# Inverse square roots on ScalarE and VectorE in place of GpSimd's power, in a two-layer macaron kernel

## The chip, the cores and the metric

The kernel runs on one core of a Trainium2 chip. Its engines work from queues of their own: TensorE (PE) multiplies matrices, VectorE (DVE) and ScalarE (ACT) do elementwise work and reductions, GpSimd (POOL) does slow elementwise work and starts indirect transfers, SyncE (SP) starts most other transfers. They meet at semaphores. The metric is the device time of one execution in microseconds (us); the time given for a kernel is the median of several runs.

## The reference

The input is 8 sequences of 256 tokens of 128 features, in float32. Six blocks follow one another, each added to the running x: a mixture of experts, attention with 16 heads, the same mixture again, a channel mix, a gated convolution and the channel mix again.

```
x = x + 0.5 * moe(layernorm(x))
x = x + attention(layernorm(x))
x = x + 0.5 * moe(layernorm(x))
x = x + 0.5 * channel_mix(layernorm(x))
x = x + gated_conv(layernorm(x))
x = x + 0.5 * channel_mix(layernorm(x))
```

The change concerns the inverse roots in it:

```
layernorm(x) = (x - mean) / sqrt(var + 1e-5)
rmsnorm(x, w) = x * rsqrt(mean(x * x) + eps) * w
out  = sum over a token's 2 experts of gate * rmsnorm(expert's row)
moe  = rmsnorm(out, out_norm_w) @ W_out.T
channel_mix: r = sigmoid(xr @ W_r); k = relu(xk @ W_k)**2; r * (k @ W_v)
gated_conv: silu for u and v, a long filter by a Fourier transform, u * o @ W_o
```

So the end of each mixture (the combine) needs, for each token, two inverse roots for the two experts' rows, and one for the sum of them; each layer norm needs one.

## The kernel before

The 2048 tokens lie in four chunks of 512 (NCH = 4), each as 4 tiles of 128 tokens (TPC = 4) across the 128 partitions, and stay in on-chip memory as `xs[c]`. Statistics of a chunk are therefore tiny tiles: 128x4 for one number a token, 128x8 for the two experts' factors `cf`.

The stages in time, as the trace has them: the first dispatch of tokens to experts, the experts of layer 0 (to about 184 us), attention's prologue (184 to 206), attention's loop, in which the dispatch of the next mixture is interleaved, the experts of the second mixture (about 419 to 517), and the tail (517 to the end), which holds the combine of the second mixture, the channel mix (`m0`), the gated convolution (`g`) and the channel mix (`m1`).

Order is written by hand. On PE, DVE, ACT and SP the instructions stand in the order in which the Python code issues them (a manual schedule); `power_of` also keeps its instructions on POOL in program order. The steps of different chunks are interleaved as closures:

- `combine` (L694) gives the steps `fetch` (transfer of the experts' rows back), `sums` (L718: cf = mean square + eps, then the power), `added` (L724: cf times gate; the first expert's rows scaled on ACT into acc, L730; the second's added on DVE, L732), `turned` (L737: transposes on PE, copy at, squares osq with row sums on ACT, L747), `produced` (L749: the sum's own inverse root ori by a power, and the matmuls with W_out), `update` (L758: x on DVE).
- `norm_sums` (L828) and `norm_rows` (L841) in attention: statistics on DVE, the power for ars, then off on DVE (L845) and the scaled rows xn_a on ACT (L853).
- `normed` (L1228) in the tail: `sums` (statistics, rs, power), `rows` (off on DVE, L1247; xn on ACT, L1252), `turned`. The channel mix goes on with `mixed` (xk and xr on ACT and DVE), `keys` (pk on PE; Relu and Square on ACT), `receptance` (pr on PE; Tanh on ACT, L1298), `values` (pkv on PE) and `update`. The gated convolution uses Silu at L1327 and L1337.

Attention's prologue works on chunk 0 in two halves of two tiles. The two lists of steps, `first` and `second`, are interleaved with a lag of two steps, and fillers (`keep_warm`, L182: matmuls whose result nobody reads) stand between PE's work. In the tail, the string `NEXT` (L53) says which chunk's next step is issued; it begins 0 1 0 2 1 0 3 0 2 1 0 2, so chunk 0's `sums`, chunk 1's `sums`, chunk 0's `added`, chunk 2's `sums`, chunk 1's `added`, chunk 0's `turned`, chunk 3's `sums`, chunk 0's `produced`, and so on.

`root_table` (L133) is a one-column Sqrt on ACT whose result nobody reads; it is called once at the start and once late in attention. The activation functions come in sets of tables, and a load (ACT_TABLE_LOAD) stands ahead of an activation whose set isn't in place. In the kernel before there are eight loads, and none in the tail.

Of the kernel before, what the change touches and what calls it, by code (L numbers as in the profile page):

```python
# [10 lines left out]
F32 = mybir.dt.float32  # L11
AF = mybir.ActivationFunctionType
# [4 lines left out]
P = 128  # L17
B, S, D = 8, 256, 128
NCH = 4
TPC = 4  # L20
# [44 lines left out]
def macaron_kernel(ctx: ExitStack, tc: tile.TileContext, a: dict, out: bass.AP):  # L65
    nc = tc.nc
# [63 lines left out]
    nc.vector.memset(zero, 0.0)  # L130
    warm = const.tile([P, 1], F32, tag="warm", name="warm")

    def root_table():  # L133
        nc.scalar.activation(warm, rms_eps, AF.Sqrt)

# [23 lines left out]

    def power_of(out, base, exponent):  # L160
        tc.keep_in_program_order(nc.gpsimd.tensor_tensor(out, base, exponent, ALU.pow))  # L161

    def bc_last(ap, n):
        return ap.unsqueeze(len(ap.shape)).to_broadcast([*ap.shape, n])
# [526 lines left out]
        with tc.If(used > len(TURNS) - NPAIR):  # L691
            work(MORE, [])

    def combine(f, c, gates, y2, mp, work=None, half=None, tiles=(0, TPC), st=None):  # L694


        t0, nt = tiles
        n = f"f{f}_{c}_{t0}"
        here, own = slice(t0, t0 + nt), range(nt)
        st = {} if st is None else st  # L700

        def work_(tag, name):
            tag = {"A": "acc", "B": "at", "C": "sq"}[tag]
            return norm.tile([P, TPC, D], F32, tag=tag, name=f"{name}_{n}")

        work = work or work_
        half = half or (lambda tag, name: bank(f"{name}_{n}", "side"))
        my = {}

        def fetch():  # L710
            if "y" not in st:
                st["y"] = mp.tile([P, 2, TPC, ROW], F32, tag="y", name=f"y_{n}", bufs=4 if f else 2)
            for k in range(2):
                r = k * NTOK + c * CT + t0 * P
                src = y2[r : r + nt * P, :].rearrange("(t p) c -> p t c", p=P)
                nc.sync.dma_start(st["y"][:, k, here], src)

        def sums():  # L718
            my["cf"] = small.tile([P, 2, nt], F32, tag="cf", name=f"cf_{n}")
            y = st["y"][:, :, here, D]  # L720
            nc.vector.tensor_scalar(my["cf"], y, 1.0 / D, RMS_EPS, ALU.mult, ALU.add)  # L721
            power_of(my["cf"], my["cf"], mhalf.unsqueeze(2).to_broadcast([P, 2, nt]))

        def added():  # L724
            y, cf = st["y"][:, :, here], my["cf"]
            at = slice(c * TPC + t0, c * TPC + t0 + nt)
            nc.vector.tensor_mul(cf, cf, gates[:, at, :].rearrange("p t k -> p k t"))
            acc = work("A", "acc")
            for t in own:
                nc.scalar.activation(acc[:, t], y[:, 0, t, 0:D], AF.Copy, scale=cf[:, 0, t : t + 1])  # L730
            for t in own:
                nc.vector.scalar_tensor_tensor(  # L732
                    acc[:, t], y[:, 1, t, 0:D], cf[:, 1, t : t + 1], acc[:, t], ALU.mult, ALU.add
                )
            my["acc"] = acc

        def turned():  # L737
            acc = my["acc"]
            pt = half("a", "pan")
            for t in own:  # L740
                nc.tensor.transpose(pt[:, ts(t, P)], acc[:, t, :], ident)
            my["at"] = work("B", "at").rearrange("p t d -> p (t d)")
            nc.scalar.copy(my["at"][:, 0 : nt * P], pt[:, 0 : nt * P])
            my["ss"] = small.tile([P, nt], F32, tag="ss", name=f"oss_{n}")
            sq = work("C", "osq")
            for t in own:
                nc.scalar.activation(sq[:, t], acc[:, t], AF.Square, accum_out=my["ss"][:, t : t + 1])  # L747

        def produced():  # L749
            ri = small.tile([P, nt], F32, tag="ri", name=f"ori_{n}")  # L750
            nc.vector.tensor_scalar(ri, my["ss"], 1.0 / D, RMS_EPS, ALU.mult, ALU.add)
            power_of(ri, ri, mhalf.to_broadcast([P, nt]))
            pp = half("b", "pout").rearrange("p (t d) -> p t d", t=TPC)
            for t in own:
                nc.tensor.matmul(pp[:, t, :], my["at"][:, ts(t, P)], wout_o, start=True, stop=True)
            my["ri"], my["pp"] = ri, pp

        def update():  # L758
            x = xs[c][:, here]
            for t in own:  # L760
                nc.vector.scalar_tensor_tensor(
                    x[:, t], my["pp"][:, t], my["ri"][:, t : t + 1], x[:, t], ALU.mult, ALU.add
                )

        return fetch, sums, added, turned, produced, update
# [25 lines left out]
    def heads(hp):  # L791
# [26 lines left out]
        def attention(mixing, leaving, filter_ends):  # L818
# [5 lines left out]
            with tc.tile_pool(name="at2", bufs=2, reuse_waits="tile") as a2:  # L824
# [3 lines left out]
                def norm_sums(c, tiles=(0, TPC)):  # L828
                    t0, nt = tiles
                    st = small.tile([P, nt, 6], F32, tag="ast", name=f"ast_{c}_{t0}")  # L830
                    mv = small.tile([P, nt, 2], F32, tag="amv", name=f"amv_{c}_{t0}")
                    for t in range(nt):
                        nc.vector.bn_stats(st[:, t, :], xs[c][:, t0 + t, :])
                    for t in range(nt):
                        nc.vector.bn_aggr(mv[:, t, :], st[:, t, :])
                    rs = small.tile([P, nt], F32, tag="ars", name=f"ars_{c}_{t0}")
                    nc.vector.tensor_scalar(rs, mv[:, :, 1], LN_EPS, None, ALU.add)
                    power_of(rs, rs, mhalf.to_broadcast([P, nt]))
                    lns[c, t0] = mv, rs

                def norm_rows(c, tiles=(0, TPC)):  # L841
# [309 lines left out]
                keep_warm(bank("warm_f", "pz"), 7)  # L1151
                for step in filter_ends:
                    step()
                warm = bank("warm_y", "sb")
                keep_warm(warm, 16)

# [14 lines left out]
                for i, step in enumerate(first):  # L1171
                    step()
                    if i >= lag:
                        second[i - lag]()
                for s in range(last + 3):
                    turn["side"] = ("sa", "pz") if s <= 1 else ("sa",)
                    new, old, older = s < last, 1 <= s <= last, 2 <= s <= last + 1
                    two = []
                    if older:
                        two.append(weights(s - 2, 1))  # L1180
                    if new:
                        two.append(scores(s, 0))
                    side_by_side(*two)
                    if older:
                        power(s - 2, 1, two[0][0])
                    if old:
                        turn_top(s - 1)
                    for step in places_[s, "a"]:
                        step()
                    turn["side"] = ("sa", "pz") if s == 0 else ("sa",)  # L1190
                    if new:
                        top(s, 0, two[-1][0])
                    two = []
                    if old:
                        two.append(weights(s - 1, 0))
                    if new:
                        two.append(scores(s, 1))
                    side_by_side(*two)
                    if old:
                        power(s - 1, 0, two[0][0])  # L1200
                    if new:
                        top(s, 1, two[-1][0])
                    if older:
                        average(s - 2)
                    for step in places_[s, "b"]:
                        step()
# [4 lines left out]
    def tail(gates, y2):  # L1211


        with (
# [12 lines left out]

            def normed(c, n):  # L1228

                st = {}  # L1230

                def sums():
                    x = xs[c]
                    bs = small.tile([P, TPC, 6], F32, tag="ast", name=f"bs_{n}_{c}")
                    mv = small.tile([P, TPC, 2], F32, tag="amv", name=f"mv_{n}_{c}")
                    for t in range(TPC):
                        nc.vector.bn_stats(bs[:, t, :], x[:, t, :])
                    for t in range(TPC):
                        nc.vector.bn_aggr(mv[:, t, :], bs[:, t, :])
                    rs = small.tile([P, TPC], F32, tag="ars", name=f"rs_{n}_{c}")  # L1240
                    nc.vector.tensor_scalar(rs, mv[:, :, 1], LN_EPS, None, ALU.add)
                    power_of(rs, rs, mhalf.to_broadcast([P, TPC]))
                    st["mv"], st["rs"] = mv, rs

                def rows():
# [157 lines left out]
            def store(c):  # L1403
                nc.sync.dma_start(out_dst[:, ts(c, TPC), :], xs[c])

            rest = [combine(1, c, gates, y2, wp, partial(work, c), partial(half, c)) for c in range(NCH)]
            for c in range(NCH):
                rest[c][0]()
            left = [
# [11 lines left out]
    def combined(f, gates, y2, gp):  # L1421

        shared = {}
        units = [combine(f, 0, gates, y2, gp, tiles=(t, 2), st=shared) for t in (0, 2)]
        units += [combine(f, c, gates, y2, gp) for c in range(1, NCH)]
        for fetch, *_ in units[:3]:
            fetch()
# [156 lines left out]
```

## Time and profile before

| what | value |
|---|---|
| time, median of 3 runs | 624.25 us (623.07 to 624.63) |
| the profiled execution | 626.05 us, of which the span from the first to the last instruction 624.1 |
| busy: PE, DVE, ACT, POOL | 522.8, 356.1, 271.0, 192.1 us |
| mean granted clock of PE | 0.969 |
| powers on POOL (L161), all | 41, of which cf 128x8 1.64 us each, 128x4 1.0, 128x2 0.7 |

How to read it: the page gives each engine's busy time, the chain of work that ended last, followed back from the last instruction, and groups of instructions with what ended the idle time ahead of them. Idle time of an engine that is not on the chain costs nothing. The granted clock says how much of TensorE's full speed it was allowed in a stretch. Between 550 and 555 us it was 0.59, between 555 and 560 0.72, and 1.00 from 524 to 550 and from 560 to 610.

Two stretches matter. In the prologue, ACT is idle from 186.79 to 193.29 us and then alternates with DVE in small steps; in the tail, the experts' rows land at 524.35 (chunk 0) and 526.74 (chunk 1), and ACT, DVE and PE work on four chunks in turn until 551.70, from where PE is busy nearly without a gap to about 598.

### The profile page before, as it was taken

The numbers are of one execution on the slowest core, as the hardware profiler recorded it, in microseconds if no ns is written. First come the engines' busy times: TensorE is split into PE (matmuls) and PEld (weight loads), VectorE is DVE, ScalarE is ACT, GpSimd is POOL, SyncE is SP. The second block draws the span as 40 slices with busy tenths as digits, with TensorE's granted clock in tenths as the row PEclk, the third lists the DMA queues.
The fourth block names the chain that finished last, engine by engine and source line by source line (L and its number), as shares of the span: only waits on it lengthen the run. The fifth ranks groups of instructions, "written<-read, shape, count | busy, mean of one in ns | idle before, by whom it ended". The sixth has DMA issues, their size and how long they took to land.

```text
span 624.1 us, 11214 instructions
## 1 busy us (share of the span) xinstructions
PE 522.8 (84%) x3879; PEld 399.4 (64%) x3879; DVE 356.1 (57%) x1108; ACT 271.0 (43%) x662; POOL 192.1 (31%) x199
## 2 busy tenths in 40 slices
PE   4531299999989999899899987669999999889996
PEld 3521188898965555556556644449999984558884
DVE  3665255554443566767876884734444442777675
ACT  3532032222332455666765564213233232876265
POOL 0567135743343121001100446402333335520110
PEclk9999999999999999999999996599999998979999
DMA  6112647767723036408111001065778745000002
GB/s 224 35 38 94 202 154 211 207 194 219 218 79 102 27 43 174 168 35 257 51 49 22 26 26 51 31 217 178 216 222 252 216 137 147 1 0 2 2 1 67
DMA packets 38122, 71.70 MB, mean 115 GB/s; under 512 B 4587, under 2 KB 27922, under 8 KB 36912
## 3 DMA queue, kind: packets, MB, share of 16 engines
q1 hardware_dynamic: 33136, 61.97, 33.3%
q0 software_dynamic: 4352, 8.47, 3.9%
q8 instruction: 32, 0.52, 0.3%
q10 hardware_dynamic: 576, 0.53, 0.2%
q14 instruction: 26, 0.21, 0.1%
HBM read 50.10 MB, written 21.38 MB: 115 GB/s over the span
## 4 chain that ended last, share of the span: by engine, by line
PE 45%; ACT 9%; DVE 7%; DMA 5%; issue 3%; SPq 1%; POOL 0%; DVEq 0%; ACTq 0%; POOLq 0%
PE ps L967 8%; PE py_f L638 4%; PE pg_f L615 4%; PE pu_f L615 4%; ACT es L1004 4%; PE po L1014 4%; DMA y<-yrow_f,idx_f 3%; PE pvf L1343 2%; PE pgo L1370 2%; PE pm L950 1%; PE pk_m L1287 1%; DVE m L987 1%; PE pkv_m L1269 1%; PE pr_m L1269 1%; DMA w_f<-in_wall_dram 1%
## 5 line engine op out<-in xcount | busy, mean ns | idle before, releaser
L658 POOL DMA_INDIRECT y<-yrow_f,idx_f x72 | 70.7, 982 | 121.2 <-issue 61.8
L1004 ACT ACTIVATE es<-ps 128x1024 f32<-128x1024 f32 x64 | 65.3, 1020 | 51.7 <-PE ps L967 29.9
L987 DVE TENSOR_REDUCE m<-pm 128x4 f32<-128x1024 f32 x64 | 77.5, 1220 | 13.2 <-PE pm L950 13.1
L967 PE MATMUL ps<-qa,qk 32*128 32x256 f32 x512 | 72.8, 401 | 12.5 <-ACT es L1004 9.6
L452 POOL DMA_INDIRECT hs<-hrow,posi_f x64 | 61.7, 964 | 64.1 <-issue 28.7
L615 PE MATMUL pg_f<-ht_f,w_f 128*128 128x256 f32 (+1 forms) x336 | 71.5, 357 | 3.4 <-DMA w_f<-in_wall_dram 2.8
L638 PE MATMUL py_f<-w_f,hg_f 128*128 128x128 f32 x576 | 71.7, 276 | 2.4 <-issue 2.4
L950 PE MATMUL pm<-qk 32*128 32x256 f32 x512 | 73.1, 400 | 0.6 <-ACT qk L897 0.6
L638 PEld LDWEIGHTS py_f<-w_f,hg_f 128*128 128x128 f32 x576 | 69.5, 192 | 4.3 <-issue 2.7
L631 DVE TENSOR_TENSOR hg_f<-pu_f,sg_f 128x1024 f32<-128x1024 f32 (+1 forms) x42 | 45.0, 1071 | 43.4 <-PE pu_f L615 36.8
L615 PE MATMUL pu_f<-ht_f,w_f 128*128 128x256 f32 (+1 forms) x336 | 69.7, 350 | 0.0
L624 ACT ACTIVATE sg_f<-pg_f 128x1024 f32<-128x1024 f32 (+1 forms) x42 | 37.9, 901 | 59.5 <-PE pg_f L615 58.9
L967 PEld LDWEIGHTS ps<-qa,qk 32*128 32x128 f32 x512 | 43.6, 184 | 30.3 <-ACT es L1004 22.5
L648 ACT ACTIVATE ysq_f<-py_f 128x128 f32<-128x128 f32 x72 | 19.3, 273 | 99.6 <-PE py_f L638 92.1
L615 PEld LDWEIGHTS pg_f<-ht_f,w_f 128*128 128x128 f32 x336 | 56.1, 194 | 9.6 <-DVE hg_f L631 1.9
L615 PEld LDWEIGHTS pu_f<-ht_f,w_f 128*128 128x128 f32 x336 | 55.2, 192 | 5.6
L950 PEld LDWEIGHTS pm<-qk 32*128 32x128 f32 x512 | 44.2, 184 | 2.5 <-issue 1.5
L649 DVE TENSOR_TENSOR yrow_f<-py_f,w_f 128x256 f32<-128x256 f32 (+1 forms) x42 | 16.2, 387 | 45.0 <-ACT ysq_f L648 44.9
L607 DVE TENSOR_SCALAR ht_f<-pht_f,pack 128x256 f32<-128x256 f32 (+1 forms) x42 | 18.6, 444 | 33.5 <-PE pht_f L605 33.5
L605 PE MATMUL pht_f<-ident,hst_f 128*128 128x128 f32 x72 | 15.4, 283 | 24.5 <-DMA hst_f<-hs 24.5
L1014 PE MATMUL po<-es,v 128*32 128x256 f32 x512 | 35.7, 393 | 0.0
L161 POOL TENSOR_TENSOR cf_f<-cf_f,mhalf 128x8 f32<-128x8 f32 (+1 forms) x9 | 13.5, 1502 | 62.9 <-DVE cf_f L721 62.0
(271 smaller groups left out, 867.7 us busy)
## 6 DMA issues: line engine op xcount, KB each, us to landing
w_f<-in_wall_dram SPq DMA_DIRECT2D x41, 832.0 KB
hs<-blank SPq DMA_DIRECT2D x8, 1032.0 KB
hst_f<-hs SPq DMA_DIRECT2D x30, 129.0 KB
y_f<-y SPq DMA_DIRECT2D x14, 258.0 KB
pack<-in_pack_dram SPq DMA_DIRECT2D x1, 1729.0 KB
heads<-qkc SPq DMA_DIRECT2D x3, 512.0 KB
qk<-heads SPq DMA_DIRECT2D x12, 128.0 KB
y<-yrow_f,idx_f POOLq DMA_INDIRECT x72
```

What stands on the lines that cost most here:

```text
L452: ins = nc.gpsimd.indirect_dma_start(out=hss[f], out_offset=bass.IndirectOffsetOnAxis(ap=st["posi"][:, t, k : k + 1], axis=0), in_=hrow[:, ...
L615: nc.tensor.matmul(ph[:, k, :], w[t][:, o + k * P : o + k * P + P], ht[t], start=True, stop=True)
L624: nc.scalar.activation(sg, pg, AF.Silu)
L631: nc.vector.tensor_mul(hg[t], pu, sg)
L638: nc.tensor.matmul(py[:, s, :], hg[t][:, k, ts(s, P)], w[t][:, 2 * DFF + k * D : 2 * DFF + k * D + D], start=(k == 0), stop=(k == NFC - 1),)
L648: nc.scalar.activation(sq[:, s], py[:, s], AF.Square, accum_out=yrow[:, s, D : D + 1])
L658: ins = nc.gpsimd.indirect_dma_start(out=y2, out_offset=bass.IndirectOffsetOnAxis(ap=idx[:, s : s + 1], axis=0), in_=yrow[:, s, :], in_off ...
L950: nc.tensor.matmul(sc[:, jj, i, :], qs[c][r, g, col + i * P : col + (i + 1) * P], ks[c][r, g, col : col + S], start=True, stop=True,)
L967: nc.tensor.matmul(sc[:, jj, i, :], ks[c][r, g, col + i * P : col + (i + 1) * P], tops[s][r, :], start=True, stop=True,)
L987: nc.vector.tensor_reduce(m, sc, AX.X, ALU.max, negate=True)
L1004: nc.scalar.activation(es, sc, AF.Exp, scale=scale)
L1014: nc.tensor.matmul(po[32 * j : 32 * j + 32, :], vs[c][:, (b % 2) * 2 + i, (g % 2) * (H // 2) + (g // 2) * 4 + j, :], ess[s, j // 2][:, j % ...
```

## The change

A helper `one_over_root` takes the root on ACT (`Sqrt`, in place) and the reciprocal on DVE (in place), or else calls `power_of` as before. It is used by table for: the six inverse roots of chunk 0 in attention's prologue (two halves, each cf, ori and ars), all four cf of the tail's combine, ori of chunks 0 to 2 there, and rs of chunks 0 and 1 in the first channel mix: 15 powers fewer on POOL, 15 Sqrt more on ACT and 15 reciprocals more on DVE. All other powers stay.

`root_table` is called twice more: after the filter's last steps ahead of the prologue, and at the start of the tail. After the prologue's steps a one-column Exp into a new tile `warm_up` follows. In the order of ACT's instructions, five table loads are new: at each of these three calls, ahead of the first Tanh in the tail (L1298, chunk 0) and ahead of the first Silu there (L1327, chunk 0). PE's and SP's orders are unchanged.

Each Sqrt and reciprocal stands where the power was issued in the program. On ACT, for the tail, this gives: Sqrt cf 0, Sqrt cf 1, acc 0, Sqrt cf 2, acc 1, at 0 and osq 0, Sqrt cf 3, Sqrt ori 0, acc 2, at 1, osq 1, at 2, osq 2, Sqrt rs 0, Sqrt ori 1, acc 3, xn 0, Sqrt ori 2, Sqrt rs 1, xk 0, xr 0, at 3, osq 3, Relu and Square of chunk 0, the load, Tanh 0.

```diff
+    def one_over_root(out, x, by_table):
+
+        if by_table:
+            nc.scalar.activation(out, x, AF.Sqrt)
+            nc.vector.reciprocal(out, out)
+        else:
+            power_of(out, x, mhalf.to_broadcast(list(x.shape)))
...
-    def combine(f, c, gates, y2, mp, work=None, half=None, tiles=(0, TPC), st=None):
+    def combine(f, c, gates, y2, mp, work=None, half=None, tiles=(0, TPC), st=None, tables=(0, 0)):
...
-            power_of(my["cf"], my["cf"], mhalf.unsqueeze(2).to_broadcast([P, 2, nt]))
+            if tables[0]:
+                one_over_root(my["cf"], my["cf"], True)
+            else:
+                power_of(my["cf"], my["cf"], mhalf.unsqueeze(2).to_broadcast([P, 2, nt]))
...
-            power_of(ri, ri, mhalf.to_broadcast([P, nt]))
+            one_over_root(ri, ri, tables[1])
...
-                    power_of(rs, rs, mhalf.to_broadcast([P, nt]))
+                    one_over_root(rs, rs, c == 0)
...
                 for step in filter_ends:
                     step()
+                root_table()
                 warm = bank("warm_y", "sb")
...
                         second[i - lag]()
+                nc.scalar.activation(warm_up, rms_eps, AF.Exp)
                 for s in range(last + 3):
...
-                    power_of(rs, rs, mhalf.to_broadcast([P, TPC]))
+                    one_over_root(rs, rs, n == "m0" and c < 2)
...
-            rest = [combine(1, c, gates, y2, wp, partial(work, c), partial(half, c)) for c in range(NCH)]
+            rest = [
+                combine(1, c, gates, y2, wp, partial(work, c), partial(half, c), tables=(1, c < 3))
+                for c in range(NCH)
+            ]
+            root_table()
...
-        units = [combine(f, 0, gates, y2, gp, tiles=(t, 2), st=shared) for t in (0, 2)]
+        units = [combine(f, 0, gates, y2, gp, tiles=(t, 2), st=shared, tables=(1, 1)) for t in (0, 2)]
```

## The prediction

> **What bounds the kernel now.** I read the chain of work that ended last first, since only what lies on it can shorten the run, and then what GpSimd (POOL) has in it, because the change takes work from POOL. The shares of the chain by engine, and the largest group of the powers:
>
> ```profile
> PE 45%; ACT 9%; DVE 7%; DMA 5%; issue 3%; SPq 1%; POOL 0%; DVEq 0%; ACTq 0%; POOLq 0%
> ...
> L161 POOL TENSOR_TENSOR cf_f<-cf_f,mhalf 128x8 f32<-128x8 f32 (+1 forms) x9 | 13.5, 1502 | 62.9 <-DVE cf_f L721 62.0
> ```
>
> A power looks dear (1.5 us), but POOL's share of the chain rounds to nothing. Next the chain in order of time over attention's prologue (start, duration, what):
>
> ```profile
> 191.58 3.70 PE warm_y L187 x8
> 195.28 0.23 PE pan_f L741 x2
> ...
> 195.80 0.70 ACT osq_f L747 x4
> ...
> 196.70 0.07 DVE cf_f L727
> ...
> 196.80 0.41 ACT acc_f L730
> ...
> 199.29 0.73 POOL ars L161
> 200.02 0.02 issue
> 200.04 0.17 DVE off L845
> 200.22 0.02 issue
> 200.24 0.89 ACT xn_a L853 x2
> ```
>
> The reader sees that the first scale factor cf (ready at 193.1) waits behind filler matmuls until 195.28, and that exactly one power of the fifteen that the change replaces, ars at 199.29, stands on the chain. The same view at the start of the tail:
>
> ```profile
> 521.97 4.76 DMA y_f<-y
> ...
> 526.84 0.17 DVE cf_f L727
> ...
> 527.08 0.41 ACT acc L730
> ...
> 532.17 1.28 ACT acc L730 x4
> ...
> 536.74 0.30 ACT acc L730
> 537.04 0.02 issue
> 537.07 0.91 DVE acc L732 x3
> ...
> 538.46 1.66 ACT xn_m L1252 x4
> ...
> 551.70 2.07 PE pk_m L1287 x2
> ```
>
> No power is in it. From the landing of the rows to 540 it runs through ScalarE (ACT) and VectorE (DVE); from 551.70 it is TensorE to the end, and those two matmuls took 2.07 us where the same pair took 1.12 at 542.64: the table by stages gives a granted clock of 0.59 between 550 and 555. Last, the prices, from the early dispatch, which already takes roots by table, and from a table load late in attention:
>
> ```profile
> L377 ACT ACTIVATE ri_f<-ri_f x7: 187/203/206, 10.0 to 394.3; 128x2 f32<-128x2 f32 x4, 128x4 f32<-128x4 f32 x3
> ```
> ```profile
> L378 DVE RECIPROCAL ri_f<-ri_f x7: 165/166/178, 10.2 to 394.5; 128x2 f32<-128x2 f32 x4, 128x4 f32<-128x4 f32 x3
> ```
> ```profile
> 383.43 1.28 ACT L134 ACT_TABLE_LOAD   x1
> 384.72 0.20 ACT L134 ACTIVATE warm<-rms_eps 128x1 f32<-128x1 f32 x1
> ```
>
> **What the Trainium skill says.** "ScalarE: Activation LUTs", section "What ACT_TABLE_LOAD costs", puts a switch of table sets at 1283 ns for the load and about 1380 ns for a drain, together 2.66 us. The trace agrees on the load (1.28 us) and shows no drain: the next activation starts 0.01 us after it. I take 1.28. Its section "Table sets: the hidden batching unit" has sqrt in a set of its own, apart from exp and tanh; so Tanh and Silu in the tail each need a load once Sqrt has displaced the set. The trace of before has no load in the tail. "TensorE: Matmul & The Clock Gate", in its paragraph on engine queue depths, calls ScalarE and VectorE strict first-in first-out; the trace agrees (cf of the first tail chunk was done on POOL at 526.32, yet its multiplication started at 526.84, behind another chunk's row sum that waited for its DMA until 526.74). The same page's Part 1 says that an idle TensorE drops to half clock in windows of about 3.4 us; the 0.59 above is such a drop.
>
> **The change, part by part.** A power costs POOL 0.7 us (2 columns), 1.0 (4) or 1.64 (8). Its replacement costs 0.04 to ACT, 0.20 sqrt, 0.02 back, 0.17 reciprocal: 0.43 us. Alone that is a gain of 0.4 to 1.3 each. But a power waited in POOL's queue, which had nothing else to do, and DVE and ACT went on with other chunks meanwhile. Now the sqrt stands in ACT's queue behind whatever the program put there, and the reciprocal stops everything behind it in DVE's queue until that sqrt is done.
>
> *Loads ahead.* The sqrt load of the prologue goes after dec (186.79), with ACT idle to 193.29: hidden. The exp load goes after the second xn_a (ends 204.94); ACT's next work is at 207.13; 1.28 plus 0.20 fits with 0.7 to spare. The tail's sqrt load falls in ACT's idle 516 to 527. All at nothing; without cover each costs up to 1.5.
>
> *Prologue.* cf of the first pair is ready 0.7 earlier: nothing, the filler ends at 195.28. cf of the second pair had its power done at 195.5, under the squares of the first pair. Now its sqrt is behind those squares on ACT: 196.41 to 196.61, reciprocal to 196.80, then the row sum of ori to 196.88, its sqrt to 197.12, its reciprocal to 197.31, the product with the gates to 197.39, and acc_f starts at 197.43, not 196.80: +0.63. Then the sqrt of ars has to wait for the second pair's squares (199.88 to 200.08), reciprocal to 200.27, and before off can go, ori's sqrt and reciprocal again (to 200.78): xn_a at 200.89 against 200.24. Sum +0.65. Nothing in the chain after it waits for an outside time, so it stays. Bounds: -0.4 (only ars' own gain) to +0.9.
>
> *Tail, first norms.* Same walk, start times on ACT, before to after:
> 1. acc of chunk 0: the product with the gates is now behind chunk 1's reciprocal (row sum ends 526.93, sqrt 527.18, reciprocal 527.37): 527.08 to 527.48, +0.40.
> 2. acc of chunk 1: behind chunk 2's round trip, whose row sum follows DVE's acc of chunk 0 at 529.07: 528.94 to 529.80, +0.86.
> 3. acc of chunk 2: the sqrts of cf 3 and ori 0 stand behind the squares of chunk 0 (end 531.86 + 0.86 = 532.72), two round trips in a row: 532.17 to 533.63, +1.46.
> 4. acc of chunk 3: ACT is full for 4.57 us from there (532.17 to 536.74 before), so to 538.2; then the round trips of rs 0 and ori 1: 536.64 to 539.13, +2.49. xn_m of chunk 0 hangs on it: 538.46 to 540.95.
> 5. xk_m of chunk 0: on ACT behind the sqrts of ori 2 and rs 1. ori 2's sqrt waits for xn_m (to 542.70), its reciprocal (to 542.89) holds chunk 1's statistics, which take 1.35 us as before, so rs 1's sqrt is at 544.20 and xk_m at 544.31, not 540.53: +3.8.
> 6. Tanh load before th_m of chunk 0: 1.28 in ACT's queue, which was full there (ka ends 545.06, th_m starts 544.96): +5.1. VectorE's update of chunk 0 and off of chunk 2 follow; xn_m of chunk 2 goes from 548.08 to about 552.28, since it had waited 1.0 us for off; so TensorE's 551.70 moves by +4.2.
> 7. Silu load before gv of chunk 0: ACT goes from xn_m straight to gv (562.10); gv is done at 562.68 and TensorE takes it at 563.10, a slack of 0.4: 1.28 - 0.4 = +0.9.
>
> Tail sum +5.1. From 563 to 598 TensorE has hardly a gap, so nothing gives it back. Bounds: +2.5 if steps 5 to 7 overlap better than I walk them, +6.5 if all of 5.1 and 1.28 add. POOL's saving of some 16.5 us of busy time (2 x 1.03, 2 x 0.69, 2 x 0.71, 4 x 1.64, 3 x 1.03, 2 x 1.01) is off the chain and worth nothing.
>
> **Sum.** The profiled execution took 626.05 (span 624.1 and 1.95 around it): 626.05 + 0.65 + 5.1 = 631.8. It was 1.8 above the median of the runs shown, 624.25; against that, 630.0.
>
> **Rivals.** About 0.3%, or 1.9 us, is what a measurement of this kernel can tell from no change.
> - *The clock gives some back.* If TensorE's activity in the shifted stretch keeps full clock, the 2.6 us lost at 551.70 to 557.2 (pk_m 0.95, pr_m 0.82, pkv_m 0.83 over their usual times) go: 627.4. For: the drop depends on where a window falls. Against: in my walk TensorE is nearly idle from 550.3 to 555.9, as long as before (546.5 to 551.7).
> - *The clock takes more.* The gaps around 540 to 546 grow, where filler matmuls barely bridged them; pk_m, pr_m, pout and pkv_m of chunk 0 (3.5 us) at half clock add up to 3.5, some 3 after overlap: 633.0.
> - *The waits are hidden anyway:* ACT and DVE have enough idle time to take 15 sqrts and 15 reciprocals (5.6 us) and two loads. 624.3. Against: ACT is busy 4.70 of 5 us between 530 and 535 and 4.45 in the next five.
> - *Faster.* One mechanism: the clock at 550 to 557. If the table's shorter latency brought pk_m of chunk 1 before the drop, 2.6 us and the 0.4 of ars would go, 621.3. It decides only if the added waits stay under 0.7 us; step 3 alone has twice that.
>
> **How the numbers follow.** Forecast 0.62 (630.0, own range 626.4 to 631.7 from the bounds of both stages together), clock gives back 0.12, clock takes more 0.13, hidden 0.08, faster 0.05. Slower 0.62 + 0.12 + 0.13 = 0.87, same 0.08, faster 0.05. The range reaches from below the first rival to the second: 626.4 to 633.0; what lies outside is hidden, faster, and half of a few in the second.
>
> **What would show it.** acc_f of the second pair near 197.4 and xn_a near 200.9; in the tail, ACT waiting for DVE's cf and DVE's reciprocals waiting for ACT's sqrts, xk_m of chunk 0 near 545 (all shifted by the 0.65), a 1.28 load before the first th_m and one before the first gv; all POOL powers of the front gone and no gain from it. It is wrong if xn_m of chunk 0 starts within 1 us of before, counted from the landing of the rows, or if TensorE's full clock holds where it dropped and the end comes earlier.

## The result and the profile after

| | before | after |
|---|---|---|
| median of 6 runs | 624.79 us (623.07 to 626.06) | 633.55 us (629.75 to 636.34) |
| ratio | | 1.0131, 95% interval 1.0097 to 1.0165 |
| profiled execution, its span | 626.05, 624.1 | 636.34, 634.6 |
| busy: PE, DVE, ACT, POOL | 522.8, 356.1, 271.0, 192.1 | 527.2, 358.6, 280.6, 175.6 |

The kernel is slower by 8.2 us (0.0131 of 624.79; 6.1 to 10.3). POOL lost 16.5 us of busy time, and nothing came of it. The chain's shares by engine, from the page of after:

```profile
PE 43%; ACT 11%; DVE 7%; DMA 6%; issue 2%; SPq 1%; POOL 0%; DVEq 0%; ACTq 0%; POOLq 0%
```

ACT rose from 9% to 11% of the chain; POOL was at 0% and is there still. Next the chain in order of time in attention's prologue (start, duration, what; L168 is the new Sqrt, L169 the new reciprocal):

```profile
197.10 0.23 PE pan_f L754 x2
...
198.32 0.10 ACT cf_f L168
...
198.95 0.17 DVE ori_f L169
...
199.21 0.41 ACT acc_f L743
...
201.67 0.20 ACT ars L168
...
202.65 0.89 ACT xn_a L866 x2
```

The root of the second pair's cf starts only at 198.32, when the squares of the first pair leave ACT; then the round trip of ori, which nobody on this path needs yet, goes first, and acc_f starts at 199.21. What the prologue waits for, the first pan_f (the transposes of the first pair on TensorE, behind the fillers), starts at 196.94 here and at 195.12 before (the timeline of PE). So acc_f comes 2.27 after it, not 1.68, and xn_a 5.71, not 5.12: +0.59.

The same view in the tail:

```profile
531.94 0.18 DVE cf_f L731
...
538.05 0.20 DVE cf_f L169
...
538.82 1.28 ACT acc L743 x4
...
546.12 1.65 ACT xn_m L1268 x4
...
549.35 0.21 ACT rs_m L168
549.56 0.58 ACT xk_m L1294
...
553.99 1.28 ACT L1314
555.28 0.60 ACT th_m L1314
...
561.06 2.08 PE pk_m L1303 x2
...
571.23 1.28 ACT L1343
572.52 0.60 ACT gv L1343
```

Between ScalarE's scaled rows (acc) small pieces of L168 and L169 now stand on the chain itself, and two table loads of 1.28 us (L1314 and L1343 without a tile). How they hold the engines up is plainest in the timeline of VectorE and of ScalarE; the bracket is the idle time ahead of the instruction and who ended it. The first line is from before, the other two are from after:

```profile
531.89 0.17 DVE L751 TENSOR_SCALAR ori_f<-oss_f 128x4 f32<-128x4 f32 x1 [1.09 <-ACT osq L747]
...
538.05 0.20 DVE L169 RECIPROCAL cf_f<-cf_f 128x8 f32<-128x8 f32 x1 [1.31 <-ACT cf_f L168]
...
549.35 0.21 ACT L168 ACTIVATE rs_m<-rs_m 128x4 f32<-128x4 f32 x1 [1.49 <-DVE rs_m L1257]
```

The 1.31 us of VectorE ahead of chunk 3's reciprocal are not all lost: before, it stood still 1.09 us at this place, for the squares of chunk 0, and its next instruction, the row sum of ori, needs these squares in any case. What is lost comes behind them. Two round trips (cf of chunk 3, ori of chunk 0) now go ahead of chunk 2's product with the gates, which needs neither: it starts 0.73 us after the squares end (538.65 and 537.92), where before it was 0.11 (531.97 and 531.86). Eleven us later ScalarE stood still 1.49 us at a root with xk_m behind it; xk_m's own input (pt_m on TensorE) was done at 548.15, so that of the time until xk_m starts at 549.46 some 1.3 us are lost. Each engine waits for the other with its queue blocked.

The starts below are counted from the row sum of chunk 1 in the tail (L721, L731), the first thing after the landing of chunk 1's rows: 526.76 before, 531.94 after. th_m is the Tanh, pk_m the matmuls of `keys`, and pvf the gated convolution's first matmuls behind its first Silu, gv.

| | before | after | difference |
|---|---|---|---|
| acc of chunk 0, of chunk 1, of chunk 2 | 0.32, 2.18, 5.41 | 0.76, 3.05, 6.88 | +0.44, +0.87, +1.47 |
| xn_m of chunk 0 | 11.70 | 14.18 | +2.48 |
| xk_m of chunk 0 | 13.77 | 17.52 | +3.75 |
| th_m of chunk 0 | 18.20 | 23.34 | +5.14 |
| pk_m of chunk 1 | 24.94 | 29.12 | +4.18 |
| first pvf | 36.18 | 41.23 | +5.05 |
| end of the last DVE instruction | 93.79 | 98.92 | +5.13 |

These are single executions. In the other profiles with before's tail (two more of before, and e1) xn_m of chunk 0 stands at 11.70 to 12.09 and the end at 92.95 to 93.98; in the other three with after's tail xn_m stands at 14.18 or 14.19 and the end at 98.38 to 99.59. In e7, whose instructions are before's up to there, xn_m stands at 12.47. So the differences hold to 0.4 to 0.8 us at xn_m, and to about 1 us at pvf and at the end.

The rest of the two profiles' difference (10.3 us) lies elsewhere: 0.59 in the prologue, 1.83 that was there already at the first filler ahead of it (185.58 and 187.41), and 2.8 net between xn_a and the landing: 5.2 more by the first activation of the second experts, since TensorE's clock fell earlier at attention's end, of which 2.5 came back in the experts. The 1.83 stand ahead of every changed instruction, and a second profile of before has this filler at 187.57 too, so they are not the change's. The experiments ask whether the 2.8 are.

### The profile page after: what moved, and what is told of

Read it like the earlier page. It is cut to its first block, busy times and chain, and to the rows that moved or that the text cites. A ratio compares the mean times of both kernels' runs of the same rounds, so it can differ in the third digit from the quotient of the medians.

```text
span 634.6 us, 11233 instructions
## 1 busy us (share of the span) xinstructions
PE 527.2 (83%) x3879; PEld 402.6 (63%) x3879; DVE 358.6 (57%) x1123; ACT 280.6 (44%) x685; POOL 175.6 (28%) x184
## 4 chain that ended last, share of the span: by engine, by line
PE 43%; ACT 11%; DVE 7%; DMA 6%; issue 2%; SPq 1%; POOL 0%; DVEq 0%; ACTq 0%; POOLq 0%
PE ps L980 8%; PE py_f L648 4%; PE pg_f L625 4%; PE pu_f L625 4%; PE po L1027 4%; ACT es L1017 3%; DMA y<-yrow_f,idx_f 3%; PE pvf L1359 2%; PE pgo L1386 2%; DMA qk<-heads 1%; PE pm L963 1%; DVE m L1000 1%; PE pk_m L1303 1%; ACT xn_m L1268 1%; PE pqk L887 1%
## 5 line engine op out<-in xcount | busy, mean ns | idle before, releaser
L1012 DVE TENSOR_TENSOR qa<-pmt,qk 128x256 f32<-128x256 f32 x32 | 13.5, 423 | 25.2 <-PE pmt L1006 25.2
```

## The experiments

**The change in halves.** In e1 the tail keeps its powers; in e2 the prologue keeps them.

```diff
 e1, against after
-                    one_over_root(rs, rs, n == "m0" and c < 2)
+                    one_over_root(rs, rs, False)
-                combine(1, c, gates, y2, wp, partial(work, c), partial(half, c), tables=(1, c < 3))
+                combine(1, c, gates, y2, wp, partial(work, c), partial(half, c), tables=(0, 0))
-            root_table()
 e2, against after
-                    one_over_root(rs, rs, c == 0)
+                    one_over_root(rs, rs, False)
-                root_table()
-                nc.scalar.activation(warm_up, rms_eps, AF.Exp)
-        units = [combine(f, 0, gates, y2, gp, tiles=(t, 2), st=shared, tables=(1, 1)) for t in (0, 2)]
+        units = [combine(f, 0, gates, y2, gp, tiles=(t, 2), st=shared, tables=(0, 0)) for t in (0, 2)]
```

> The changed prologue alone; the tail takes powers on GpSimd as before. Theory (queues couple): xn_a starts 0.65 us later than before, counted from warm_f, the loads are hidden, and the run is 0.65 us longer: about 625.4 against 624.8. Rival A (the roots by table help here): 0.4 us shorter, the one power on the chain. Rival B (any shift ahead of attention moves TensorE's clock drop at its end into busier work): +0.65 and up to 3.7 more, as the profiled run of the changed kernel lost between 373 and 394 us, so up to 629.

> The changed tail alone; attention's prologue as before. Theory: +5.1 us, 629.9; counted from the landing of chunk 1's rows, xn_m of chunk 0 is 2.5 us later than before, pk_m of chunk 1 4.2, pvf of chunk 0 5.1. Rival B: nothing ahead of the tail is shifted, so the excess of the changed kernel over its forecast (about 2.5 us) must be absent here; if it is here too, it comes from the tail or from chance.

Measured: e1 1.0007 (0.9983 to 1.0031), pan_f to xn_a 5.71, xn_m of chunk 0 at 11.98 and the end at 93.98. e2 1.0111 (1.0079 to 1.0144), pan_f to xn_a 5.13, xn_m at 14.19, th_m at 23.35, pk_m of chunk 1 at 29.13, the end at 98.83. Each half shows in its trace what after shows there, and the two don't meet. e1's ratio leaves no room for the full 3.7 us more of its rival B. The prologue's +0.59 is below what its ratio can tell from zero; that it is there rests on the traces. The tail carries the loss: its ratio is +6.9 us (4.9 to 8.9), where the trace counts 5.0.

**The tail's loads and its round trips apart.** e3 is the kernel before with the root's table loaded at the tail's start, so that Tanh and Silu have to load theirs, and no root moved. e4 is e2 with Copy, an activation for which its trace has no load in the tail, in place of the root: the trips stay, the roots and the loads are left out.

```diff
 e3, against before
+            root_table()
 e4, against e2
-            nc.scalar.activation(out, x, AF.Sqrt)
+            nc.scalar.activation(out, x, AF.Copy)
-            root_table()
```

> The kernel before with one more root_table at the start of the tail, so that Tanh and Silu need their loads; every power stays on GpSimd. Theory: the load before th_m of chunk 0 delays TensorE's pk_m of chunk 1 by only 0.4 us, because xn_m of chunk 2 had waited 1.0 us for off; the one before gv costs 0.9: together +1.3, 626.1. Rival (loads are the whole loss): +5.1. Rival (loads hidden): 0.

> The changed tail alone with Copy in place of Sqrt and without root_table there, so that the trips over ScalarE and back stay and no table is loaded in the tail; the roots are left out of what is computed. Theory (waits in the queues are the larger part): +4.0, 628.8; xn_m of chunk 0 2.5 us later than before from the landing, xk_m of chunk 0 3.8. Rival (loads are the loss): under +0.5.

Measured: e3 1.0031 (1.0011 to 1.0052), e4 1.0088 (1.0056 to 1.0120). The chain of e3 in order of time has the loads in their places:

```profile
542.21 1.28 ACT L1298
543.51 0.60 ACT th_m L1298
...
559.22 1.28 ACT L1327
```

From the row sum, e3 has th_m at 19.61 (+1.41), pk_m of chunk 1 at 25.39 (+0.45), pvf at 37.26 (+1.08), the end at 94.95 (+1.16). So TensorE feels 0.45 of the first load and the second brings it to 1.1. e4 has xn_m at 14.20 and xk_m at 17.54, both as in after, th_m at 21.95 (+3.75), the end at 97.49 (+3.70). The parts add up: 3.70 + 1.16 = 4.86, against 5.04 for both in e2; counted from the mean end of the four profiles with before's tail (93.45) they are 4.0 and 1.5, against 5.4. Either way about three quarters of the tail's loss are the trips between two in-order queues, their waits and the pieces' own time, and would be there if the tables were free.

**After again.** The kernel after was run once more, unchanged, beside the kernel before.

> The changed kernel as it is, measured again beside its control. Theory: tail +5.1 and prologue +0.6 in the trace, so +5.7, a ratio of 1.009; what the first measurement had above that (1.0131) came from where TensorE's clock drops elsewhere in the run, and averages out. Rival: the excess is the change's own, and the ratio is 1.013 again.

Measured: 1.0112 (1.0081 to 1.0143), which is 6.9 us of 618.4 (5.0 to 8.8). The interval holds the theory's 1.009 and the rival's 1.013, so the ratio does not decide between them. In its trace xn_a comes 5.70 after pan_f, xn_m, th_m and pk_m of chunk 1 stand at 14.18, 23.34 and 29.13, and the end at 98.38.

**Is it the reciprocal's place?** e6 is after with each reciprocal moved down to where its result is first used, so that VectorE doesn't stop at it; the roots stay.

```diff
 e6, against after
             nc.scalar.activation(out, x, AF.Sqrt)
-            nc.vector.reciprocal(out, out)
...
+            if tables[0]:
+                nc.vector.reciprocal(cf, cf)
             nc.vector.tensor_mul(cf, cf, gates[:, at, :].rearrange("p t k -> p k t"))
...
+            if tables[1]:
+                nc.vector.reciprocal(my["ri"], my["ri"])
             for t in own:
...
+                    if c == 0:
+                        nc.vector.reciprocal(rs, rs)
...
+                    if n == "m0" and c < 2:
+                        nc.vector.reciprocal(st["rs"], st["rs"])
```

> The changed kernel with each of the 15 reciprocals moved from right behind its Sqrt to right ahead of its use (cf in the step that multiplies with the gates, ori in the update, ars and rs in the rows), so that VectorE no longer stands still for ScalarE; Sqrts, loads and their places on ScalarE as before. Theory (half of the loss is VectorE's standing still): prologue from +0.6 to about -0.1; in the tail, from the landing, xn_m of chunk 0 +1.0 instead of +2.5, xk_m of chunk 0 +1.8 instead of +3.8, pvf of chunk 0 +3.2 instead of +5.0; run +3.1. Rival (the Sqrt's place in ScalarE's queue is what counts): no change, +5.7.

Measured: 1.0068 (1.0043 to 1.0093), that is +4.2 us (2.7 to 5.8). xn_m of chunk 0 stands at 12.81 (+1.11, where after has +2.48), xk_m at 15.51 (+1.74), pvf at 38.74 (+2.56), the end at 96.43 (+2.64); in the prologue xn_a comes 5.26 after pan_f (+0.14). At the place in VectorE's timeline where chunk 3's reciprocal stood, the row sum of ori is now the first, and chunk 2's reciprocal follows without a wait:

```profile
527.94 0.17 DVE L765 TENSOR_SCALAR ori_f<-oss_f 128x4 f32<-128x4 f32 x1 [1.22 <-ACT osq L761]
528.02 0.19 DVE L740 RECIPROCAL cf_f<-cf_f 128x8 f32<-128x8 f32 x1
```

The idle time is now that of the row sum of ori, which waits for the squares themselves, as before the change. So the place of the reciprocals cost some 2.0 us in the tail of e6 against e2 (from +2.49 to +1.11 at xn_m, from +3.76 to +1.74 at xk_m). What is left up to xk_m, 1.7, I put down to the roots standing in ScalarE's queue and to the reciprocals' own time; no run takes these two apart.

**TensorE's clock in the tail.** The prediction saw 2.6 us lost to half clock at pk_m of chunk 1. In e7 the kernel before gets fillers of 4 and 7 blocks of 128 columns into the gap ahead of it, and in e8 after gets the same.

```diff
 e7, against before; e8, against after
                 keep_warm(warm, WARM.get(i, 0))
+                if i in (31, 33):
+                    keep_warm(half(NCH - 1, "a", f"warm_{i}"), 4 if i == 31 else 7)
```

> The kernel before with eleven filler matmul blocks more (4 behind the transposes of chunk 1's first channel mix, 7 behind chunk 2's), in the stretch where TensorE is nearly idle ahead of its half clock at pk_m of chunk 1. Theory (that stretch's idleness drops the clock, and it costs 2.6 us): pk_m, pr_m and pkv_m of chunk 1 at full clock, 1.1 instead of 2.07 for pk_m, and the run 2.6 us shorter. Rival (the drop is set by something else): same durations, no gain.

> The changed kernel with the same eleven filler blocks. Theory: the same 2.6 us off, so +3.1 against the kernel before; the waits in the tail ahead of pk_m of chunk 1 stay as they are. Rival (the clock is part of the changed kernel's excess): more than 2.6 off.

Measured: e7 0.9958 (0.9936 to 0.9980), or 2.6 us faster than before; e8 1.0099 (1.0073 to 1.0125). PE's timeline of e7, where the pair took 2.07 in before:

```profile
545.48 1.12 PE L1287 MATMUL pk_m<-xk_m,pack 128*128 128x512 f32 x2
546.45 1.05 PE L1269 MATMUL pr_m<-pack,xr_m 128*128 128x128 f32 x8
```

The clock holds, and e7 beats both kernels; from xn_m of chunk 0 its trace ends 2.2 us earlier than the first profile of before, and 1.1 to 2.2 earlier than the four profiles with before's tail (the three of before, and e1). In e8 th_m and pk_m of chunk 1 keep the delays of after (22.57 and 28.36 from acc of chunk 0, against 22.58 and 28.36), and the end comes 1.87 earlier than in the first profile of after, 1.33 earlier than in e5's. So the change's waits up to there are no matter of the clock. That the fillers make after faster too, as forecast, its runs do not show: e8's ratio is 6.1 us (4.5 to 7.7), where 3.1 was expected, and its median, 625.36, is close to that of after in the same series, 625.49 (e5). Its trace, counted against the first profile of before like the other kernels, gives 3.9 (3.26 at the end and 0.59 in the prologue); that gap stays open.

**Attention's end, and chance.** In the first profile of after, the clock fell some us earlier at attention's end than in that of before. Either the change does that, or it varies by itself. Two more profiles of before and a third of after (e5 has the second) were taken, and e9 adds to e7 fillers into the last steps of attention.

```diff
 e9, against e7
+                def filled(n, name):
+                    return lambda: keep_warm(bank(f"warm_{name}", "px"), n)
+                    filled(6, "34a"),
+                    filled(2, "34b"),
+                    filled(2, "34c"),
+                    filled(2, "34d"),
+                    filled(16, "34e"),
+                for s_, h_ in ((31, "b"), (32, "a"), (32, "b"), (33, "a"), (33, "b")):
+                    at(s_, h_, filled(4, f"{s_}{h_}"))
```

> The kernel before, unchanged, for a second profile of it. Theory (the clock's drop at attention's end falls by chance from run to run): its time from es 44 to the first sg of the second experts differs from the first profile of before by over 1 us, so that +3.7 us there is no part of the change. Rival (the change sets the drop): within 0.5 us of the first profile. In the tail, pk_m of chunk 1 at half clock (about 2.07) and the end of DVE 93.8 us after chunk 1's row sum in both.

> As look_before_1, a third profile of the kernel before: the same two readings.

> The changed kernel, unchanged, a third profile of it. Theory: counted from chunk 1's row sum, xn_m of chunk 0 +2.5, th_m +5.1, pvf +5.0 as in the two profiles before, and prologue +0.6; the time from es 44 to the first sg of the second experts is within the spread of the profiles of before. Rival (the change sets the clock's drop at attention's end): that time is 2 us or more above all profiles of before.

> The kernel before with the tail's fillers of e7 and, besides, fillers of 4 blocks in the last five half steps of attention's loop and of 2, 6 and 16 blocks in the steps after it (all into the bank px). Theory: at the end of attention TensorE drops to about half clock because its small matmuls leave it too little activity; fillers hold the clock, the first sg of the second experts comes up to 3 us earlier than in e7, and the run is 0.5 to 0.9% faster than before. Rival: the clock drops there for another reason, or the bank px is still read when a filler wants it, so the fillers stand on TensorE's path: as e7 (0.996) or slower by up to 3 us (1.000).

Measured, all counted from the first es of attention's loop, in us (es is attention's exponential, sg the experts' first activation on ScalarE):

| | before | before, second | before, third | after | e5 | after, third | e9 |
|---|---|---|---|---|---|---|---|
| last es | 165.82 | 165.98 | 168.98 | 169.58 | 165.68 | 165.82 | 167.93 |
| first sg of the second experts | 199.87 | 200.43 | 205.08 | 205.04 | 199.20 | 198.02 | 201.97 |
| row sum of chunk 1 in the tail | 312.80 | 312.04 | 318.41 | 315.51 | 310.61 | 310.68 | 314.15 |

In the third profile of before the clock falls as early as in after's first profile, and in the two other profiles of after it doesn't. From the tables by stage, one line of before's third profile and then one of its first, both 162 us after the first es; the columns are the stretch, its length, the busy time and count of PE, weight loads, DVE, ACT and POOL, then the granted clock, and last the DMA share and GB/s:

```profile
375.10:377.10 2.00, 2.00 (x21) 0.85 (x19) 0.94 (x6) 1.02 (x1) 1.14 (x2) 0.67 0.15 41
```
```profile
376.00:378.00 2.00, 1.89 (x24) 1.32 (x14) 0.46 (x4) 0.78 (x1) 1.26 (x2) 1.00 0.15 45
```

So the early drop comes without the change and stays away with it. Nor do all thirteen profiles without fillers there show that the change makes it likelier: from the first es to the row sum of chunk 1, the seven with before's attention take 309.4 to 318.4 us, 313.4 in the mean, and the six with after's 310.6 to 315.5, 313.2 in the mean. The 2.8 us are chance. The theory did not hold in each of its points: the second profile of before stays within 0.6 us of the first at the first sg, and the end was forecast 93.8 after the row sum in both, where it stands at 92.95 and 93.07. In the third profile of after the prologue again has 5.71 and xn_m 14.18, but th_m stands at 24.28 and the end at 99.59, for in that execution the clock fell ahead of chunk 0's pk_m. PE's timeline:

```profile
544.97 2.07 PE L1303 MATMUL pk_m<-xk_m,pack 128*128 128x512 f32 x2 [0.57 <-DVE xk_m L1297]
```

e9 gave 0.9972 (0.9950 to 0.9993), no better than e7: the rival. The clock was 1.00 in every stretch of 2 us from 372.4 to 400.4, yet the last es came 2.1 later than in before, and from there the first sg took 34.04, where before took 34.05 with the clock at 0.50 from 382. In the loop the five fillers, about 1.0 us each, stand between TensorE's own matmuls. After the loop e9 does not show that the clock sets no pace, since its fillers there take TensorE's time as well. The thirteen profiles without fillers do not settle it: from the last es to the first sg the five in which the clock had fallen by 164 us after the first es take 33.8 to 36.1 us, the other eight 32.2 to 34.5.

## Why the prediction was right

*What bounds the kernel.* That POOL is off the chain, and its saving worth nothing, held: 16.5 us fewer busy, chain at 0% as before.

*Loads ahead.* Hidden, all three. The prologue's load ran at 188.63; the Exp load at 207.43 ended with its activation at 208.92, and ACT's next work began at 209.60, 0.7 later, as worked out; the tail's at 522.29 lay in ACT's idle time before the first rows landed (chunk 0's row sum starts at 529.81). From xn_a to the first es it took 13.72 before and 13.78 after.

*Prologue.* Forecast +0.65, measured +0.59 in all three profiles of after and in e1. acc_f of the second pair took nearly all of it, by the round trip of ori in front, as said. The gain at ars, whose power is gone, and the waits behind it cancelled.

*Tail, steps 1 to 7.* Every step measured within 0.05 us of its forecast in the pair of first profiles, where the walk began; that it fits so closely at the end, +5.13 for +5.1, is in part luck, since the means of the profiles give 5.5. e3, e4 and e6 show that it is also for the reasons given: without loads th_m loses the 1.4 of the first and keeps the 3.75 of the trips; with the reciprocals late the trips shrink to 1.7. Step 7 put a slack of 0.4 between gv and TensorE; by the timelines the half of it is there (gv +5.24, pvf +5.05), and the other half lies ahead of gv, which moved 1.06 more than pk_m of chunk 1 and not 1.28. Both are below what varies between executions at pvf.

*The Trainium skill.* "ScalarE: Activation LUTs", section "What ACT_TABLE_LOAD costs", names a drain beside the load. Taking 1.28 alone was right: th_m starts 1.29 us after its load does (553.99 and 555.28). The page's 1.38 on top would have put some 2.8 on th_m in e3, which has +1.41. The strict queues of "TensorE: Matmul & The Clock Gate" are the mechanism of the larger part of the loss, and e6 shows it: the same instructions in another place of the queue cost 2.0 us less at xk_m.

*The rivals.* "Hidden" and "faster" fell. "The clock gives some back" didn't come: pk_m of chunk 1 took 2.08 in all three profiles of after. "The clock takes more" came in one of them, the third, through the gap named, but not at its price: th_m lost another 0.94 and the end 0.67 to 1.21 against the other two, for the clock came back earlier later on, where 3 was forecast.

*The size.* The sum of 5.75 is what the traces show (5.7 in the first profiles, 6.1 with the means of three profiles of each kernel's tail and those of e1 and e2). The forecast of 630.0 was nevertheless 3.5 below the first median, 633.55, which lies just above the range's end of 633.0 (the measured ratio on the 624.25 from which the forecast starts gives 632.4). The term mis-sized is in "How the numbers follow": the range took its bounds from the prologue and the tail alone, and the clock only in the tail. Most of what moves between executions lies ahead of the tail: from the first es to chunk 1's row sum the same kernel before took 312.0 to 318.4 us, and with six runs that can go into the median. Run again, the difference was 6.9 (5.0 to 8.8), which holds 5.75 and 6.1, and the first measurement's 8.2 too. Not settled: the ratios of the kernels with the changed tail lie some 1.4 to 2.5 us above the sums of their own traces (e2 6.9 and 5.0, e4 5.4 and 3.7, e6 4.2 and 2.8, e8 6.1 and 3.9, the first runs of after 8.2 and 5.7). The sums of e2, e4, e5 and e6 are inside the ratios' intervals, those of e8 and of the first runs of after just below. Some 0.3 of the gap comes from the first profile of before, whose end (93.79) is later than the mean (93.45). Executions such as the third profile of after may explain another part; how often they occur no run counts.

## What to carry to other kernels

A slow engine with an empty queue can be the cheapest place for a small operation: of fifteen powers of 0.7 to 1.6 us on an idle GpSimd only one, of 0.73 us, stood on the chain, while nine round trips of some 0.43 us each between ScalarE and VectorE cost 3.7 us in the tail, because a wait in an in-order queue stops all that stands behind it. When an operation must be split over two engines, put its second half just before its use (2.0 us back here), and price the table loads at the place where the displaced set is needed again, not only where the new one is loaded. And look for the same loss in what is already there: fillers for one gap that crossed into half clock made the kernel before 0.4% faster.

## What the runs showed that I had not expected

- The clock at attention's end falls at different places in executions of one and the same kernel: in before at 380 to 382 us, in its third profile already in the stretch 375.1 to 377.1, with TensorE busy 2.00 of 2.00 us there. In that execution the last es came 3.2 us later and the landing 5.6. The Trainium skill, "TensorE: Matmul & The Clock Gate", Part 1, says that the window in which activity is judged runs freely, so that the point of change varies, by half a microsecond in its case; the three profiles agree that it varies, but by up to 8 us (162, 166 and 170 us after the first es), and no run here shows the window.
- Fillers that held the clock at 1.00 through attention's end (e9) gained nothing there: the last es came 2.1 us later, and the time from it to the first sg stayed at 34.04 us, for 34.05.
- Half clock costs less than it seems when it comes and goes: chunk 0's pk_m and pr_m at 2.07 and 1.91 us, for 1.12 and 1.05, left 0.67 to 1.21 us at the end.
